# Reordering one slot and the tail of a 16-batch graph-attention kernel: turns of x1, projections, row-sum reciprocal and flag load

## The chip, the core and the metric

The kernel runs on one core of one Trainium2 chip. The metric is device time in microseconds (us) of one launch; less is better. Each time below is the median of its runs, or belongs to one profiled execution where that is said.

## The reference

There are 16 batches of 1024 rows with 256 features in float32, and a 0/1 adjacency matrix of 1024 x 1024 for each. Two layers follow each other, each with a residual and a layernorm. Cut to what matters here (the adjacency holds 0 and 1 only, so one of the four kinds of edge of layer 0 is used):

```python
# layer 0
e0    = leaky(einsum('bid,bjd->bij', h * a0[:, 0], h))      # slope 0.2
alpha = sigmoid(where(adj == 1, e0, -max))                  # kinds 2, 3, 4 likewise, with a1, a2, a3
x     = layernorm(x + einsum('bij,bjd->bid', alpha, h) + bias)
# layer 1
Hh     = einsum('bni,io->bno', x, W)
s, d   = Hh @ a_src, Hh @ a_dst
e      = where(adj != 0, exp(-leaky(s[:, :, None] + d[:, None, :])), 0)
rowsum = where(sum(e, -1) == 0, 1, sum(e, -1))
x      = layernorm(x + elu(einsum('bnm,bmo->bno', e, Hh) / rowsum))
```

## The kernel before

`one_kind_pass` does the work for an adjacency of zeros and ones. On the way it counts, in the tiles `chk` and `fit`, whether that assumption held; at the end the counts become one integer, `flag`, every engine loads it into a register, and `general_pass`, a second program for other adjacencies, runs behind `tc.If(n_bad > 0)`. Here it never runs: every engine takes the branch past it.

The order of work on each engine is the order in which the lines are written (`tc.manual_schedule`, line 79). Each engine runs its queue strictly in that order, and waits at an instruction whose input is not there; the queue of SP, which issues nearly all transfers, and the queue of POOL work in the same way. So "moved up" means: put ahead of other instructions of the same queue.

A batch of 1024 rows is 8 tiles of 128. Per batch there are these pieces:

- `strip(b, jt)` (line 191): scores of row tile jt against the tiles from jt on (the matrix is symmetric), on TensorE (PE) into a PSUM tile `pe`, then two tanh on ScalarE (ACT, lines 213 and 214) into `tb` (four buffers) and `low` (two buffers), and their maximum on VectorE (DVE, line 215).
- `finish` (line 217) masks the strip into `al`. `dump` (line 233) transposes the strip in blocks of 32 x 32 on DVE (line 237) and writes it to device memory in 4 transfers (line 241); `gather` (line 243) reads it back as the mirrored half; `mask` (line 249) masks that half (line 252).
- `sum0(b, t)` (line 305): 8 matmuls of `al` against `x` for one row tile, then bias and statistics on DVE. `center` gives the layernorm's scale and offset on POOL: `rstd` (line 276, six small operations, one of them a power) and two operations more (`mr`, lines 296 and 297). `scale0` applies them on ACT (line 301), giving the new x1.
- `save_x1(b, g)` writes one half (512 rows) of x1 to device memory (line 338); `fetch_x1(b, g)` reads it back in 32-column blocks with 8 transfers (line 112); `turn_x1(b, g)` transposes 32 x 32 blocks in place on DVE (line 349). Together they give x1 transposed, `x1T`.
- `project(b, t)` (line 351): `x1T` times `W` on PE (line 365), then three ACT operations (lines 373 to 375). Tiles 0 to 3 need the first half of x1T, tiles 4 to 7 the second. `share_p` and `weights` (line 409, on DVE) build the attention weights `e`.
- `sum1(b, t, acc, m)` (line 416): one matmul of 8 for a row tile of layer 1. `elu(b, t)` (line 424) takes the row sum out of PSUM, makes its reciprocal on DVE (lines 431, 433, 434) and applies it on ACT (lines 436, 437); `add` (line 439) adds the residual and takes statistics on DVE; `scale1` normalizes on ACT (line 301), `store` writes out (line 451).

The batches overlap in slots. Slot b (line 491) holds first the 8 strips of batch b with the 8 projections of batch b-1 between them, then 8 `sum0` of batch b, then 8 `sum1` of batch b-1. Batch 0's strips and `sum0` come before the loop, so slot 1, the second, is the only one whose previous batch has its x1 saved and fetched just before, and it has its own order: line 498 says which projections follow which strip, lines 501 to 511 where scale0, save, fetch and turn of batch 0 stand.

```python
            projects = [[], [], [], [], [0, 1], [2, 3], [], [4, 5, 6, 7]]
            if prev == 0 and jt in (3, 6):
                turn_x1(0, (jt - 3) // 3)
```

In the other slots the two turns of batch b stand at `t == 4` of the `sum1` loop and after that loop (line 580). After the loop over slots, lines 585 to 629 finish the last batch: three row tiles of `sum1` are accumulated together, m by m, as the weights come (lines 587 to 595); five more follow one by one; layernorm and stores are cut into pieces of 3, 3 and 2 tiles. Line 981 loads the flag.

## Time and profile before

| what | us |
|---|---|
| median of 3 runs | 1307.55 (1306.74 to 1307.65) |
| the profiled execution's own time | 1307.63 |
| its span in the profile | 1305.8 |
| TensorE busy in the span | 1268.1 (97%) |
| VectorE busy | 941.3 (72%) |
| ScalarE busy | 652.5 (50%) |
| GpSimd (POOL) busy | 304.2 (23%) |

The span is 1.8 us shorter than the time of the run it was taken in. In the profile PE is TensorE, and PEld its weight loads, which overlap the matmuls; DVE is VectorE, ACT ScalarE, and a q behind an engine's name its sequencer, which waits, branches and issues transfers. The granted clock of TensorE is 0.99 over the span. A busy share of 97% is a mean over stages: the first 6 us and the last 16 us hold no matmul of the loop, and the rest of the idle time lies in few places.

### The profile page before, as it was taken

The numbers are of one execution on the slowest core, as the hardware profiler recorded it, in microseconds if no ns is written. First come the engines' busy times: TensorE is split into PE (matmuls) and PEld (weight loads), VectorE is DVE, ScalarE is ACT, GpSimd is POOL, SyncE is SP. The second block draws the span as 40 slices with busy tenths as digits, with TensorE's granted clock in tenths as the row PEclk, the third lists the DMA queues.
The fourth block names the chain that finished last, engine by engine and source line by source line (L and its number), as shares of the span: only waits on it lengthen the run. The fifth ranks groups of instructions, "written<-read, shape, count | busy, mean of one in ns | idle before, by whom it ended". The sixth has DMA issues, their size and how long they took to land. (4 is left out here: it accounts for less than half of the span.)

```text
span 1305.8 us, 17594 instructions
## 1 busy us (share of the span) xinstructions
PE 1268.1 (97%) x5445; PEld 1024.2 (78%) x5445; DVE 941.3 (72%) x2126; ACT 652.5 (50%) x1461; POOL 304.2 (23%) x608
## 2 busy tenths in 40 slices
PE   7979999999999999999999999999999999999995
PEld 5758788787887878788787887878788787887874
DVE  5566786868868686786868868687786868768664
ACT  4543544645445464545645445464445635446434
POOL 2213121322212223121322213223121322213213
PEclk9989999999999999999999999999999999999998
DMA  9385497694857948488594866958488594866201
GB/s 215 64 179 108 89 193 143 128 194 84 183 122 166 186 91 192 90 182 160 114 201 84 191 121 144 195 95 201 81 181 170 111 196 76 194 135 140 72 15 68
DMA packets 609158, 181.30 MB, mean 139 GB/s; under 512 B 486184, under 2 KB 591648, under 8 KB 609056
## 3 DMA queue, kind: packets, MB, share of 16 engines
q1 hardware_dynamic: 588464, 138.61, 48.9%
q0 software_dynamic: 20592, 41.48, 17.9%
q8 instruction: 46, 0.75, 0.2%
q14 instruction: 56, 0.46, 0.1%
HBM read 152.44 MB, written 61.14 MB: 164 GB/s over the span
## 5 line engine op out<-in xcount | busy, mean ns | idle before, releaser
L312 PE MATMUL acc<-x,al 128*128 128x256 f32 x2048 | 449.3, 380 | 5.2 <-DVE al L252 5.2
L416 PE MATMUL acc<-H,e 128*128 128x257 f32 x2048 | 448.7, 380 | 1.4 <-DVE e L409 1.4
L312 PEld LDWEIGHTS acc<-x,al 128*128 128x128 f32 x2048 | 386.4, 190 | 62.7 <-DVE al L252 10.8
L416 PEld LDWEIGHTS acc<-H,e 128*128 128x128 f32 x2048 | 387.9, 190 | 59.3 <-DVE e L409 2.2
L205 PE MATMUL pe<-xa,xT 128*128 128x384 f32 (+3 forms) x768 | 267.8, 487 | 0.0
L205 PEld LDWEIGHTS pe<-xa,xT 128*128 128x128 f32 x768 | 142.2, 190 | 87.4 <-issue 45.9
L301 ACT ACTIVATE x<-x,mr,r 128x256 f32<-128x256 f32 x128 | 69.2, 592 | 231.4 <-POOL mr L297 231.4
L280 POOL TENSOR_SCALAR ve<-mv 128x4 f32<-128x4 f32 (+3 forms) x51 | 17.7, 347 | 699.0 <-DVE mv L274 698.8
L409 DVE SCALAR_TENSOR_TENSOR e<-p,pq,adj 128x1024 f32<-128x1024 f32 x128 | 159.7, 1270 | 20.1 <-DMA p<-p_row 17.2
L436 ACT ACTIVATE h<-acc,rinv 128x256 f32<-128x256 f32 x128 | 60.2, 470 | 202.5 <-DVE rinv L434 191.8
L213 ACT ACTIVATE tb<-pe 128x512 f32<-128x512 f32 (+1 forms) x192 | 94.3, 491 | 109.6 <-PE pe L205 80.0
L365 PE MATMUL pH<-Wx,x1T 128*128 128x258 f32 x512 | 131.1, 392 | 7.6 <-DVE x1T L349 4.3
L431 DVE COPY rs<-acc 128x1 f32<-128x1 f32 x128 | 20.2, 158 | 162.1 <-PE acc L416 161.6
L365 PEld LDWEIGHTS pH<-Wx,x1T 128*128 128x128 f32 x512 | 100.4, 197 | 45.2 <-issue 14.0
L215 DVE TENSOR_TENSOR tb<-tb,low 128x512 f32<-128x512 f32 (+1 forms) x192 | 101.8, 543 | 45.4 <-ACT low L214 24.6
L120 ACT ACTIVATE junk<-adj,minus 128x2048 bf16<-128x2048 bf16 x64 | 127.3, 1990 | 0.0
L231 POOL TENSOR_TENSOR al<-ident,al 128x128 f32<-128x128 f32 x128 | 60.0, 472 | 212.3 <-DVE al L221 212.1
L221 DVE SCALAR_TENSOR_TENSOR al<-tb,adj 128x512 f32<-128x512 f32 (+7 forms) x132 | 97.5, 739 | 5.0
L320 DVE SCALAR_TENSOR_TENSOR x<-acc,bias_bc 128x256 f32<-128x256 f32 x128 | 54.0, 422 | 62.4 <-PE acc L312 62.2
L214 ACT ACTIVATE low<-pe 128x512 f32<-128x512 f32 (+1 forms) x192 | 93.2, 485 | 0.8 <-DVE tb L215 0.8
L282 POOL TENSOR_TENSOR r<-ve,power 128x4 f32<-128x4 f32 (+3 forms) x51 | 79.2, 1552 | 4.2
L237 DVE STREAM_TRANSPOSE tb<-tb 128x896 f32<-128x896 f32 (+6 forms) x105 | 74.7, 712 | 3.6
(62 smaller groups left out, 938.0 us busy)
## 6 DMA issues: line engine op xcount, KB each, us to landing
adj<-in_adjT POOLq DMA_DIRECT2D x30, 1024.0 KB, 9.5
x_rows<-x SPq DMA_DIRECT2D x32, 512.0 KB, 3.4
x1T<-x_rows SPq DMA_DIRECT2D x256, 64.0 KB, 2.4
x<-in_x SPq DMA_DIRECT2D x15, 1024.0 KB, 5.8
xT<-in_x SPq DMA_DIRECT2D x120, 128.0 KB, 3.5
out<-y SPq DMA_DIRECT2D x30, 512.0 KB, 3.8
p<-p_row POOLq DMA_DIRECT2D x15, 512.0 KB, 4.2
mir<-tb SPq DMA_DIRECT2D x60, 112.0 KB, 2.4
```

Source lines behind the costliest of these rows:

```text
L120: nc.scalar.activation(junk, rows, AF.Square, bias=minus1, scale=2.0, accum_out=chk[:, b * CHECKS + n : b * CHECKS + n + 1],)
L205: nc.tensor.matmul(pe[:, 0:w], lhsT=xTs[b][:, c, ts(jt, P)], rhs=xas[b][:, c, ds(jt * P + o, w)], start=(c == 0), stop=(c == ND - 1),)
L213: nc.scalar.activation(tb[:, ds(o, w)], pe[:, 0:w], AF.Tanh, scale=0.5)
L214: nc.scalar.activation(low[:, 0:w], pe[:, 0:w], AF.Tanh, scale=0.5 * SLOPE)
L215: nc.vector.tensor_tensor(tb[:, ds(o, w)], tb[:, ds(o, w)], low[:, 0:w], ALU.max)
L221: nc.vector.scalar_tensor_tensor(als[b][:, jt, c0:c1], tbs[b, jt][:, c0 - jt * P : c1 - jt * P], 1.0, adjs[b, jt // HT][:, jt % HT, c0:c1] ...
L237: nc.vector.transpose(tb, tb)
L282: nc.gpsimd.tensor_tensor(r, ve, power[:, 0:n_t], ALU.pow)
L312: nc.tensor.matmul(acc, lhsT=als[b][:, jt, ts(t, P)], rhs=xs[b][:, jt, :], start=(jt == 0), stop=(jt == NT - 1),)
L365: nc.tensor.matmul(pt, lhsT=x1Ts[b][:, c, ts(t, P)], rhs=Wx[:, c, :], start=(c == 0), stop=(c == ND - 1),)
L409: nc.vector.scalar_tensor_tensor(es[b][:, m, :], p_bcs[b], pqs[b][:, m, 1:2], adjs[b, m // HT][:, m % HT, :], ALU.mult, ALU.min)
L416: nc.tensor.matmul(acc, lhsT=es[b][:, m, ts(t, P)], rhs=Hs[b][m], start=(m == 0), stop=(m == NT - 1),)
```

## The change

In slot 1 the first turn of x1 goes ahead of the first strip, scale0 and save of the second half go from after the second strip to after the first, and projections 0 to 3 go to one each behind strips 1 to 4. In all other slots but the last, the second turn goes from after the `sum1` loop to its step 6. The row sum is no longer copied out of PSUM: one maximum with a tiny constant reads it there. In the last batch four row tiles are accumulated together in place of three, one weights step moves behind the step it was ahead of, the flag is computed at step 5 of the last loop, its load stands ahead of the last store, the last tile's relu and normalization are done on VectorE, so that its two `mr` operations on POOL fall away, and its store is split in two.

```diff
+    TINY = 1.0e-36
-        rs = small.tile([P, 1], F32, tag="rs", name=f"rs_{b}_{t}")
-        nc.vector.tensor_copy(rs, acc[:, D : D + 1])
         rinv = small.tile([P, 1], F32, tag="rinv", name=f"rinv_{b}_{t}")
-        nc.vector.scalar_tensor_tensor(rinv, rs, 0.0, rs, ALU.is_equal, ALU.add)
+        nc.vector.tensor_scalar(rinv, acc[:, D : D + 1], TINY, None, ALU.max)
         nc.vector.reciprocal(rinv, rinv)
-        nc.scalar.activation(hs[b, t], acc[:, 0:D], AF.Relu, scale=rinv)
+        if (b, t) == (B - 1, NT - 1):
+            nc.vector.tensor_scalar(hs[b, t], acc[:, 0:D], rinv, 0.0, ALU.mult, ALU.max)
+        else:
+            nc.scalar.activation(hs[b, t], acc[:, 0:D], AF.Relu, scale=rinv)
...
-            projects = [[], [], [], [], [0, 1], [2, 3], [], [4, 5, 6, 7]]
+            projects = [[], [0], [1], [2], [3], [], [], [4, 5, 6, 7]]
+            turn_x1(0, 0)
         for jt in range(NT):
             strip(b, jt)
-            if prev == 0 and jt == 1:
+            if prev == 0 and jt == 0:
                 for t in range(HT, NT):
                     scale0(0, t)
                 save_x1(0, 1)
...
-            if prev == 0 and jt in (3, 6):
-                turn_x1(0, (jt - 3) // 3)
+            if prev == 0 and jt == 6:
+                turn_x1(0, 1)
...
             if last and t == 7:
                 weights(b, 0)
-                weights(b, 1)
             elu(prev, t, acc)
             if last and t == 7:
-                weights(b, 2)
+                weights(b, 1)
...
+            if not last and t == 6:
+                turn_x1(b, 1)
...
         if not last:
-            turn_x1(b, 1)
             add(prev, NT - 1)
...
-    first = [acc1(last, t, ps_e, "e") for t in range(3)]
+    n_first = 4
+    first = [acc1(last, t, *((ps_e, "e") if t < 3 else (ps_t, "t"))) for t in range(n_first)]
     for m in range(NT):
-        if m >= 3:
+        if m >= 2:
             weights(last, m)
...
+    nc.vector.tensor_reduce(any_bad, bad, AX.X, ALU.max)
+    flag = const.tile([1, 1], I32, tag="flag", name="flag")
...
+        if t == 5:
+            total = ps_t.tile([P, HT, P], F32, tag="t", name="total")[0:1, 0, 0:1]
+            nc.tensor.matmul(total, lhsT=any_bad, rhs=ones, start=True, stop=True)
         elu(last, t, acc)
...
+        if t == 5:
+            nc.vector.tensor_copy(flag, total)
...
+    t = NT - 1
+    add(last, t)
+    for q in range(3, t):
         scale1(last, q)
         if q == 5:
             store(last, 3, 3)
-    r1s[last] += center(mv1s[last][:, 7:8, :], f"1_{last}_7")
-    scale1(last, 7)
-    store(last, 6, 2)
+        elif q == 6:
+            store(last, 6, 1)
+    mv = mv1s[last][:, t : t + 1, :]
+    r = rstd(mv, f"1_{last}_{t}")
+    n_bad = nc.values_load(
+        flag, min_val=0, max_val=P, skip_runtime_bounds_check_because="a number of partitions"
+    )
+    y = ys[last][:, t, :]
+    nc.vector.tensor_scalar(y, y, mv[:, 0, 0:1], r, ALU.subtract, ALU.mult)
+    store(last, t, 1)
+    return n_bad
```

The computation of the flag is taken out of `tile_adj_resnorm_kernel` with this.

More of the change, by code (lines that the diff above doesn't have):

```diff
@@ L41, in one_kind_pass @@
     fit: bass.AP,
-):
+) -> bass.RuntimeValue:
     nc = tc.nc
@@ L139, in one_kind_pass @@
     nc.vector.memset(minus1, -1.0)
+    ones = const.tile([P, 1], F32, tag="ones", name="ones")
+    nc.vector.memset(ones, 1.0)
     warm = const.tile([P, 1], F32, tag="warm", name="warm")
@@ L593, in one_kind_pass @@
             r1s[done] = center(mv1s[done], f"1_{done}")
-        for t in range(3):
+        for t in range(n_first):
             sum1(last, t, first[t], m)
     check_pq(last)
+    n_chk, n_fit = chk.shape[1], fit.shape[1]
+    bad = const.tile([P, n_chk + n_fit], F32, tag="bad", name="bad")
+    nc.vector.tensor_scalar(bad[:, 0:n_chk], chk, float(NT * N // CHECKS), None, ALU.is_gt)
+    nc.vector.tensor_scalar(bad[:, n_chk:], fit, 0.5, None, ALU.is_lt)
+    any_bad = const.tile([P, 1], F32, tag="any_bad", name="any_bad")
+    nc.vector.tensor_reduce(any_bad, bad, AX.X, ALU.max)
+    flag = const.tile([1, 1], I32, tag="flag", name="flag")
     for t in range(NT):
-        if t < 3:
+        if t < n_first:
             acc = first[t]
@@ L606, in one_kind_pass @@
             add(last, t - 1)
+        if t == 5:
+            nc.vector.tensor_copy(flag, total)
         if t == 6:
             add(last, t)
-        if t in (3, 6):
-            r1s[last] += center(mv1s[last][:, ds(t - 3, 3), :], f"1_{last}_{t - 3}")
-        if t == 7:
-            add(last, t)
+        if t in (4, 6):
+            r1s[last] += center(mv1s[last][:, ds(0 if t == 4 else 3, 3), :], f"1_{last}_{t}")
         if t == 6:
@@ L622, in one_kind_pass @@
             store(last, 0, 3)
-    for q in range(3, 7):
+    t = NT - 1
+    add(last, t)
+    for q in range(3, t):
         scale1(last, q)
@@ L967 @@
         fit = flagp.tile([P, B], F32, tag="fit", name="fit")
-        one_kind_pass(tc, x, adjT, a0, bias, W, a, out, chk, fit)
-        with tc.tile_pool(name="flag_ps", bufs=1, space=PSUM) as flag_ps:
-            bad = flagp.tile([P, NCHK + B], F32, tag="bad", name="bad")
-            nc.vector.tensor_scalar(bad[:, 0:NCHK], chk, float(N // P * N // CHECKS), None, ALU.is_gt)
-            nc.vector.tensor_scalar(bad[:, NCHK:], fit, 0.5, None, ALU.is_lt)
-            any_bad = flagp.tile([P, 1], F32, tag="any_bad", name="any_bad")
-            nc.vector.tensor_reduce(any_bad, bad, AX.X, ALU.max)
-            ones = flagp.tile([P, 1], F32, tag="one", name="one")
-            nc.vector.memset(ones, 1.0)
-            total = flag_ps.tile([1, 1], F32, tag="total", name="total")
-            nc.tensor.matmul(total, lhsT=any_bad, rhs=ones, start=True, stop=True)
-            flag = flagp.tile([1, 1], I32, tag="flag", name="flag")
-            nc.vector.tensor_copy(flag, total)
-        n_bad = nc.values_load(flag[0:1, 0:1], min_val=0, max_val=P)
+        n_bad = one_kind_pass(tc, x, adjT, a0, bias, W, a, out, chk, fit)
         with tc.If(n_bad > 0):
```

## The prediction

> **What bounds the kernel now.** I read the page's busy shares first, then the waits of PE, then the timelines of the two places where PE waits, and last the end of the span on POOL. Everything is taken from one profiled execution of 1307.63 us (span 1305.8, so 1.8 us lie around it); the median of the runs is 1307.55, the same within 0.08. I give the new time on the scale of 1307.63.

> ```profile
> PE 1268.1 (97%) x5445; PEld 1024.2 (78%) x5445; DVE 941.3 (72%) x2126; ACT 652.5 (50%) x1461; POOL 304.2 (23%) x608
> ...
> PE acc L312 <- DVE al L252: 5.2, 14, 0.4
> PE pH L365 <- DVE x1T L349: 4.3, 1, 4.3
> PE pH L365 <- DMA mir<-tb: 3.1, 1, 3.1
> ...
> PE acc L416 <- DVE e L409: 1.4, 2, 0.9
> ```

> PE has 97%, so DVE, ACT or POOL work taken away elsewhere is worth nothing unless PE waits for it. It waits in four ways that the change can touch: 0.4 us in each of 14 slots (L252), 4.3 and 3.1 us once each in slot 1, and 1.4 us in the m-loop of the tail. The first one stays: the mask follows a strip that waits for PE itself (DVE is idle for 1.86 us at 639.1 before L215), so a shorter DVE queue does not bring it forward.

> Slot 1 on PE's timeline (start, length, operation, count, idle before):

> ```profile
> 58.29 13.12 PE L205 MATMUL pe<-xa,xT 128*128 128x512 f32 x36
> 75.72 3.63 PE L365 MATMUL pH<-Wx,x1T 128*128 128x258 f32 x8 [4.31 <-DVE x1T L349]
> ...
> 86.76 6.65 PE L365 MATMUL pH<-Wx,x1T 128*128 128x258 f32 x16 [3.06 <-DMA mir<-tb]
> 93.73 0.28 PE L391 MATMUL prow<-ident,pq 128*8 128x128 f32 x1 [0.32 <-ACT pq L374]
> ```

> Strips and projections take 58.29 to 93.85, 35.6 us, against 22.6 us (621.51 to 644.09) in a slot of the middle: 13 us are lost here. The second wait is named after a transfer, but what ends last is the turn of the second half on DVE (L349, 85.35 to 86.55). Beside the idle time there is the clock, in PE's windows (us, busy, granted clock, DMA share, GB/s):

> ```profile
> 77.00:78.00 1.00, 1.00 (x3) 0.50 0.75 114
> ...
> 90.00:91.00 1.00, 1.00 (x4) 0.50 0.72 179
> ```

> The clock is halved for 3.4 us from 75.6 and for 6.8 us from 85.9, so the 16 matmuls at 86.76 take 6.65 us; the same 16 at full clock take 3.75 (1252.13). Then SP's queue:

> ```profile
> 66.23 2.17 SPq L241 DMA_DIRECT2D mir<-tb  x4
> 68.50 0.55 SPq L338 DMA_DIRECT2D x_rows<-x  x1
> 69.41 2.61 SPq L241 DMA_DIRECT2D mir<-tb  x4
> 72.11 4.26 SPq L112 DMA_DIRECT2D x1T<-x_rows  x8
> 76.47 0.43 SPq L245 DMA_DIRECT2D al<-mir  x1
> 77.01 3.14 SPq L241 DMA_DIRECT2D mir<-tb  x4
> ```

> From 66.23 it issues without a pause. It is to be seen that 17 transfers stand between the start of dump 1 and the end of dump 2, and that they fill the time up to 80.15.

> At the end, POOL:

> ```profile
> 1288.44 0.32 POOL L280 TENSOR_SCALAR ve<-mv 128x3 f32<-128x3 f32 x1 [6.79 <-DVE mv L274]
> ...
> 1296.49 0.19 POOL L296 TENSOR_TENSOR mr<-mv,r 128x1 f32<-128x1 f32 x1
> 1296.76 0.23 POOL L297 TENSOR_SCALAR mr<-mr 128x1 f32<-128x1 f32 x1
> ...
> L981 POOLq TENSOR_LOAD <-flag x1: 498/498/498, 1296.7 to 1296.7; - x1
> ...
> L982 POOLq INC_SWDGE_SEM  x1: 632/632/632, 1302.5 to 1302.5; - x1
> ```

> POOL works without a pause from 1288.44 to 1296.99 (three chains of a layernorm), loads the flag, branches at 1297.33 and only goes on at 1299.96; after 1302.5 come a drain (to 1305.0) and the barrier. SP has seen the last store land at 1300.8 and waits for POOL. POOL sets the end; the last store has 2.2 us to spare.

> [...]

> **Row sum (L431 to L434).** 128 copies of 158 ns fall away, 20.2 us of DVE, and the compare with two sources becomes a maximum from PSUM, a read like the copy's. In the slots DVE is not what PE waits for, so nothing follows. In the tail it is 0.2 us on the way to POOL.

> **turn_x1(b, 1) at step 6 of sum1.** The same 1.25 us operation in 14 slots, two steps earlier, ahead of the DVE part of the last two elu. DVE is idle for about 1.47 us just there (620.24 to 621.71). It waits for the fetch behind it; the last landing comes 1.65 us before in slot 1, 1.98 in slot 3, 2.4 to 4.5 in the others. Cost 0.

> **Slot 1.** *First turn.* It stands ahead of strip 0 in DVE's queue. Its fetch (8 transfers of L112 from 53.92) has landed by 60.83, and DVE's timeline has nothing from 59.6 to 61.33: turn from 60.95 to 62.2, the second L215 starts at 63.04 as before, the first is late by 0.9 us without anyone waiting. Cost 0. With it projections 0 to 3 run between the strips at full clock; the 4.31 us of idle time and the slow 3.63 us are gone, but PE then reaches the end of its strips at about 77.5 and stands still until the second turn. So only the second turn counts. *scale0* (four on ACT, 2.06 us) starts when POOL has the offsets, 63.24, to 65.35, ahead of tanh operations that then come late: dump 1 becomes ready about 0.46 us later, 69.87. *save* then runs at 65.4 in a free stretch of SP instead of in the full one. Dump 1 takes 2.1 (a middle slot, 633.52 to 635.62) to 2.6 us. The fetch behind it so shifts by s = -0.05 to +0.46. *Then* the same 17 transfers; dump 2's last landing moves from 82.24 to 82.24 + s. The buffer `tb` is one of four, so tanh of strip 6 waits for that landing: 82.4 + s, against 83.29 now, when PE's slow projections held it. From there to the turn DVE takes what it takes now (tanh at 83.29, turn at 85.35), less about 0.2 since mask 0 is done by then: PE starts at 82.4 + 0.2 + 3.1 = 85.6 to 86.1 against 86.76, a gain of 0.65 to 1.15; I take 0.8. *Clock*: PE has then idled for 8 us and starts cold. It leaves half speed after 3.4 to 6.8 us[...]: the 16 matmuls take 3.5 + half of that, 5.2 to 6.7, middle 5.95, against 6.65: -0.7. Together -1.5, bounds -0.4 to -2.6.

> **Tail, PE.** Four accumulators instead of three mean 4 x 0.435 us of matmuls per m, so that `e` (L409, 1.27 us each) is due later. Laid out again with the durations of the DVE rows, the second `e` (now behind the elu's reciprocal, 1260.32 to 1261.59) is 0.04 us late and the third (behind add, 1262.98 to 1264.25) 0.92, 0.96 together, where the same count gives 1.83 now (0.56 and 0.87 by the record, the rest inside the groups); with 0.1 for the flag's matmul, which goes from behind the last row tile to ahead of it, the last row tile ends 0.75 us earlier. **Tail, POOL.** Its chain for tiles 3 to 5 starts with row tile 5's add, so 0.75 + 0.2 (row sum) earlier, and stays without a pause; the last two `mr` operations fall away (1296.49 to 1296.99, less the overlap with the load: 0.54). The branch comes 1.5 us earlier. [...] **Tail, DVE.** Tile 7's relu on DVE reads PSUM: 0.42 us (by L442, two sources), against 0.47 on ACT; POOL needs tile 7's statistics at 1293.5, and has them at about 1291.5. [...] I take 0.42 against 0.60 on ACT: store at about 1295.95, seen by SP at about 1299, 2.6 us ahead of POOL. Cost and gain 0, and none for splitting the store. The flag's load on the other engines stands in waits for POOL's r. Sum -1.5.

> **Sum:** 1307.63 - 1.5 - 1.5 = 1304.6.

> **Rivals.** *A, slot 1 gives nothing*: the queue of SP is later than I think[...]: 1307.63 - 1.5 = 1306.1. For it: the same transfers, a clock that depends on chance. Against it: tanh 6 was held by PE, not by SP. *B, SP was not the limit*: once PE no longer delays strips 4 to 6, transfers land faster, and the second turn follows its own fetch (landed by 78.2) more closely, some 5 us earlier: 1299.6. Against it: dump 2 issues without a pause. *C, slower*: turn_x1(b, 1) at step 6 stands ahead of the elu of the last row tiles; if its fetch lands late in the slots, DVE's queue waits, and after it strip 0's L215 and PE. It has 1.65 us or more of margin, and DVE 1.86 us of idle time at strip 4, so it decides from about 4.2 us of delay; 5 us late in 14 slots would give 14 x 0.8 = 11, thus about 1316. For it: nothing in the landing times; only that removed DVE work and earlier turns could bunch the transfers.

> **How the numbers follow.** Forecast 0.73, A 0.12, B 0.08, C 0.07. A measurement of this kernel tells 0.2% (2.6 us) from no change, that is 1304.9. The forecast's own range is 1303 to 1306.4; a little over half of it, 0.44, lies below 1304.9. Faster 0.44 + 0.08 = 0.52, same 0.29 + 0.12 = 0.41, slower 0.07. The range takes in A and POOL's gap: 1302.4 to 1307.2; B and C are left out.

> **What would show it.** Right: in slot 1 no wait before projections 0 to 3, one wait of about 8 us before 4 to 7 that begins at about 77.5, PE at 85.6 to 86.1, sum0 at 91.5 to 92.8 instead of 93.85; slots of 78.7 us as now; POOL's branch 1.5 us earlier against the last matmul's old place, and POOL still last. Wrong: L349 waiting on L112 in the slots, sum0's start near 89 or after 93.8, or the last store behind POOL.

## The result, and the profile after

The changed kernel takes 1303.37 us (median of 10 runs, 1302.71 to 1304.77) against 1307.18 (10 runs, 1306.02 to 1308.07) for the kernel before on the same chip: 3.8 us less, ratio 0.9973 with a 95% interval of 0.9963 to 0.9982. The forecast was 1304.6.

The profiled execution of the changed kernel was the longest of its ten: 1304.77, span 1303.0. It is 2.86 us shorter than the profiled one of before, not 3.8; what differs from execution to execution is found below. Lines were added to its code, so the numbers have moved, many by three: L312 is L315 now, L365 is L368, L409 is L412, L349 is L352, L241 is L244; the fetch, L112, is L113.

The waits of PE (line, releaser, us in total, times, longest):

```profile
PE pH L368 <- issue: 8.4, 1, 8.4
...
PE acc L315 <- DVE al L255: 5.3, 14, 0.4
...
PE acc L419 <- DVE e L412: 0.6, 1, 0.6
```

The two waits of slot 1 (4.3 and 3.1) have become one of 8.4 us. The 14 waits in front of sum0 are untouched, and of the tail's two waits one is left. PE's timeline of slot 1:

```profile
63.74 1.03 PE L368 MATMUL pH<-Wx,x1T 128*128 128x258 f32 x4
...
72.97 1.03 PE L368 MATMUL pH<-Wx,x1T 128*128 128x258 f32 x4
73.85 2.76 PE L208 MATMUL pe<-xa,xT 128*128 128x384 f32 x12
85.05 6.54 PE L368 MATMUL pH<-Wx,x1T 128*128 128x258 f32 x16 [8.45 <-issue]
91.92 0.28 PE L394 MATMUL prow<-ident,pq 128*8 128x128 f32 x1 [0.33 <-ACT pq L377]
92.03 3.25 PE L315 MATMUL acc<-x,al 128*128 128x256 f32 x14
```

Projections 0 to 3 run between the strips at full clock (4 instructions, two for each matmul, in 1.03 us), PE is through with the strips at 76.6, and then stands still until projections 4 to 7. sum0 starts at 92.03 instead of 93.85, of which 0.99 us were there before slot 1 began (first strip at 57.30 instead of 58.29). The wait is put down to "issue", so it is DVE's timeline that says what ended it:

```profile
77.54 0.45 DVE L240 STREAM_TRANSPOSE tb<-tb 128x256 f32<-128x256 f32 x1
79.85 1.16 DVE L255 SCALAR_TENSOR_TENSOR al<-al,adj 128x384 f32<-128x384 f32 x2 [1.87 <-DMA al<-mir]
82.60 0.42 DVE L218 TENSOR_TENSOR tb<-tb,low 128x256 f32<-128x256 f32 x1 [1.58 <-ACT low L217]
83.06 0.42 DVE L224 SCALAR_TENSOR_TENSOR al<-tb,adj 128x256 f32<-128x256 f32 x1
83.51 0.31 DVE L240 STREAM_TRANSPOSE tb<-tb 128x128 f32<-128x128 f32 x1
83.75 1.20 DVE L352 STREAM_TRANSPOSE x1T<-x1T 128x1024 f32<-128x1024 f32 x1
```

The turn (L352) is ready to run at 77.6, when the last block of its fetch lands, and DVE is idle from 77.98 to 79.85 and again from 81.0 to 82.6. It runs at 83.75, because strip 6 stands ahead of it and waits for its buffer (ACT's L216 of strip 6 starts at 81.91, after 5.70 us of waiting for `mir<-tb`). SP's queue, where the buffer's release comes from, is full as before:

```profile
64.98 0.38 SPq L341 DMA_DIRECT2D x_rows<-x  x1
65.45 6.07 SPq L244 DMA_DIRECT2D mir<-tb  x8
71.57 4.31 SPq L113 DMA_DIRECT2D x1T<-x_rows  x8
75.98 0.43 SPq L248 DMA_DIRECT2D al<-mir  x1
76.51 3.12 SPq L244 DMA_DIRECT2D mir<-tb  x4
```

The save now stands ahead of dump 0, and dumps 0 and 1 follow each other. The fetch starts at 71.57 instead of 72.11; counted from the first strip that is 14.27 us instead of 13.82, so in this execution it is later, not earlier. At the end, POOL (its timeline, then the operations of the branch's line, with their shortest, middle and longest duration in ns):

```profile
1285.46 0.32 POOL L283 TENSOR_SCALAR ve<-mv 128x3 f32<-128x3 f32 x1 [4.17 <-DVE mv L277]
...
1293.40 0.19 POOL L291 TENSOR_TENSOR r<-r,n 128x1 f32<-128x1 f32 x1
```

```profile
L998 POOLq EVENT_SEMAPHORE  x5: 17/43/43, 1296.9 to 1299.5; - x5
...
L998 POOLq COMPARE_BRANCH  x1: 45/45/45, 1293.9 to 1293.9; - x1
...
L998 POOLq INC_SWDGE_SEM  x1: 636/636/636, 1299.6 to 1299.6; - x1
```

The last two operations of the chain are gone and POOL branches at 1293.92 instead of 1297.29, 3.4 us earlier; but from there to the semaphore operation (INC_SWDGE_SEM) it takes 5.69 us instead of 5.19. Cut into stretches, the two profiled executions compare so (us, from PE's and POOL's instructions in the traces; the last matmul, counted to its end, is that of row tile 7):

| stretch | before | after | difference |
|---|---|---|---|
| start to first strip of slot 1 | 58.29 | 57.30 | -0.99 |
| slot 1, first strip to sum0 | 35.55 | 34.73 | -0.82 |
| a middle slot (mean of 12) | 78.689 | 78.683 | -0.006 |
| last slot, its strips to projections 0 to 3 of batch 15 | 72.10 | 71.90 | -0.20 |
| projections 4 to 7 of batch 15 to the last matmul | 37.65 | 36.96 | -0.69 |
| last matmul to POOL's branch | 7.51 | 6.93 | -0.58 |
| branch to INC_SWDGE_SEM | 5.19 | 5.69 | +0.50 |
| from there to the end | 3.36 | 3.37 | 0 |

### The profile page after: what moved, and what is told of

Same layout as the page of the kernel before. It is cut to its first block, busy times and chain, and to the rows that moved or that the text cites. A ratio compares the mean times of both kernels' runs of the same rounds, so it can differ in the third digit from the quotient of the medians.

```text
span 1303.0 us, 17447 instructions
## 1 busy us (share of the span) xinstructions
PE 1265.0 (97%) x5445; PEld 1022.0 (78%) x5445; DVE 925.4 (71%) x2000; ACT 650.7 (50%) x1459; POOL 295.3 (23%) x606
## 4 chain that ended last, share of the span: by engine, by line
PE 82%; issue 5%; SPq 4%; DVE 4%; DMA 3%; POOL 1%; ACT 1%; POOLq 0%; DVEq 0%
PE acc L315 34%; PE acc L419 30%; PE pe L208 13%; PE pH L368 4%; SPq L244 3%; DMA mir<-tb 2%; DVE al L224 1%; DVE tb L240 1%; DVE tb L218 1%; ACT tb L216 1%; DVE al L255 1%; POOL r L285 1%; ACT low L217 0%; DMA x<-in_x 0%; SPq L248 0%
## 5 line engine op out<-in xcount | busy, mean ns | idle before, releaser
L315 PE MATMUL acc<-x,al 128*128 128x256 f32 x2048 | 449.3, 380 | 5.3 <-DVE al L255 5.3
L315 PEld LDWEIGHTS acc<-x,al 128*128 128x128 f32 x2048 | 386.4, 190 | 62.8 <-DVE al L255 10.9
L412 DVE SCALAR_TENSOR_TENSOR e<-p,pq,adj 128x1024 f32<-128x1024 f32 x128 | 159.8, 1270 | 20.8 <-DMA p<-p_row 17.8
L216 ACT ACTIVATE tb<-pe 128x512 f32<-128x512 f32 (+1 forms) x192 | 94.3, 491 | 117.2 <-PE pe L208 78.5
L368 PE MATMUL pH<-Wx,x1T 128*128 128x258 f32 x512 | 129.4, 387 | 8.5 <-issue 8.4
L435 DVE TENSOR_SCALAR rinv<-acc 128x1 f32<-128x1 f32 x128 | 20.1, 157 | 162.2 <-PE acc L419 162.1
L368 PEld LDWEIGHTS pH<-Wx,x1T 128*128 128x128 f32 x512 | 99.1, 194 | 45.5 <-issue 22.9
L234 POOL TENSOR_TENSOR al<-ident,al 128x128 f32<-128x128 f32 x128 | 68.2, 533 | 241.2 <-DVE al L224 241.0
L255 DVE SCALAR_TENSOR_TENSOR al<-al,adj 128x512 f32<-128x512 f32 (+3 forms) x150 | 76.5, 534 | 1.9 <-DMA al<-mir 1.9
```

The costliest lines, as they stand in the source:

```text
L216: nc.scalar.activation(tb[:, ds(o, w)], pe[:, 0:w], AF.Tanh, scale=0.5)
L255: nc.vector.scalar_tensor_tensor(v, v, 1.0, rows, ALU.add, ALU.mult)
L315: nc.tensor.matmul(acc, lhsT=als[b][:, jt, ts(t, P)], rhs=xs[b][:, jt, :], start=(jt == 0), stop=(jt == NT - 1),)
L368: nc.tensor.matmul(pt, lhsT=x1Ts[b][:, c, ts(t, P)], rhs=Wx[:, c, :], start=(c == 0), stop=(c == ND - 1),)
L412: nc.vector.scalar_tensor_tensor(es[b][:, m, :], p_bcs[b], pqs[b][:, m, 1:2], adjs[b, m // HT][:, m % HT, :], ALU.mult, ALU.min)
```

## The experiments

All were timed in five rounds beside the kernel before, whose median was 1306.96, 1306.88 and 1307.09 in the three groups.

**Slot 1 alone, and everything else alone.**

```diff
-            projects = [[], [], [], [], [0, 1], [2, 3], [], [4, 5, 6, 7]]
+            projects = [[], [0], [1], [2], [3], [], [], [4, 5, 6, 7]]
+            turn_x1(0, 0)
...
-            if prev == 0 and jt == 1:
+            if prev == 0 and jt == 0:
...
-            if prev == 0 and jt in (3, 6):
-                turn_x1(0, (jt - 3) // 3)
+            if prev == 0 and jt == 6:
+                turn_x1(0, 1)
```

This on the kernel before:

> The kernel before with the three edits of slot 1 alone (first turn ahead of strip 0, scale0 and save behind strip 0, projections 0 to 3 behind strips 1 to 4). Theory (slot 1 is worth the earlier second turn only, the clock little): slot 1 from its first strip to sum0 takes 34.7 us instead of 35.6, time 0.5 to 1.5 us below before, and the tail's POOL branch stands against the last matmul as in before. Rival (all of the 3.8 us comes from slot 1): 3 us or more below before.

1304.94 us, ratio 0.9984 (0.9977 to 0.9991): about 2 us, more than the 0.5 to 1.5 expected and less than the rival's 3. Slot 1 takes 32.84, not 34.7. The reverse of this diff on the changed kernel:

> The changed kernel with the order of slot 1 put back. Theory: keeps the gain of the tail, about 0.7 on PE, 0.6 on POOL and 0.2 in the last slot[...]: 1.2 to 2.2 us below before, and slot 1 at 35.6 us. Rival (slot 1 is all): as before. Rival (parts help each other): more than 3 us below before.

1305.69, ratio 0.9991 (0.9983 to 0.9999): 1.3 us; slot 1 at 35.58. So about 2 us are slot 1 and 1.3 the rest, and they add up to the whole within the noise (3.2 us for the changed kernel in the same rounds, next).

**The changed kernel again.**

> The changed kernel once more, to see what differs from execution to execution. Theory: the 1.0 us by which its first profile was ahead of before's at the first sum0, before any edit acts, and the 0.5 us by which POOL's gaps behind its branch were longer, are chance: one or both come out different here by 0.2 us or more, while slot 1 (34.7), the middle slots (78.68) and the stretch from the last strips to the last matmul (37.0) agree within 0.3. Rival: the changed program starts faster because it is shorter or laid out otherwise: first sum0 at 24.5 again, and gaps of 2.9 and 2.4 again.

1303.78, ratio 0.9977 (0.9966 to 0.9987). The first strip of slot 1 is at 58.09 this time, so the head start of 1 us is chance. The fetch of slot 1 begins at 71.57 in one execution and 71.59 in the other, so the first had lost its head start again by then. POOL's stretch from the branch to INC_SWDGE_SEM is 5.51 again (5.69 in the first), so that it is longer than before is not chance. Slot 1 does not agree, against what was expected: 33.00 against 34.73, sum0 at 91.09 against 92.03. The middle slots (78.68) and the stretch to the last matmul (36.95) do. PE's windows of the two (us, busy, granted clock, DMA share, GB/s), first the one profiled first, then this one:

```profile
85.00:88.00 3.00, 2.95 (x7) 0.50 1.06 225
88.00:91.00 3.00, 3.00 (x9) 0.54 0.49 102
91.00:92.00 1.00, 0.68 (x4) 1.00 0.32 82
```

```profile
85.00:88.00 3.00, 3.00 (x8) 0.50 1.05 216
88.00:89.00 1.00, 1.00 (x4) 0.50 0.27 48
89.00:90.00 1.00, 1.00 (x6) 0.96 0.87 204
```

In the first the clock is half from 80.53 to 90.77, three times 3.41 us; in this one from 82.26 to 89.08, twice 3.41. PE begins at 85.05 and 84.83, so it works at half speed for 5.7 us in the one and 4.3 in the other. At a clock of 0.50 half of that difference, 0.7 us, is lost time. The other 1.0 of the 1.73 us came earlier: PE began 27.75 us after the first strip in the first execution and 26.74 in this one, since the save, and behind it the fetch, were later there (7.68 and 14.27 us after the first strip, against 6.70 and 13.50). The first profile had the worse draw in both.

The kernel before varies too. Of its 98 executions in the five rounds, 87 took 1305.9 to 1308.9 us and 11 took 1303.6 to 1304.1, these at a mean clock of 0.994 instead of 0.991 or 0.992. So one execution in nine of the old kernel is as short as the new one, and only medians of many tell them apart. Less time at half clock would fit the higher mean, but none of the eleven was profiled.

**Is it scale0 and the save?** One edit put back in the changed kernel:

```diff
-            if prev == 0 and jt == 0:
+            if prev == 0 and jt == 1:
                 for t in range(HT, NT):
```

> The changed kernel with scale0 and the save of the second half back behind strip 1; the first turn and the projections stay where the change puts them. Theory (the second turn comes earlier because PE's slow projections no longer hold strip 6, and the moved save spares SP 0.5 us at most): projections 4 to 7 still begin at 84.5 to 85.8 us of the span, sum0 at 90.4 to 92.8, within 1 us of the changed kernel. Rival (scale0 and save moved up are what brings the fetch and so the turn forward): projections 4 to 7 at 86.5 or later, and 2 us or more above the changed kernel.

1304.14 (ratio 0.9982, 0.9975 to 0.9989), projections 4 to 7 at 84.20, 27.05 us after the first strip and so among the other executions, sum0 at 89.84. Moving scale0 and save brings nothing that can be measured; the first turn and the projections, taken together, do it: strip 6 no longer stands behind slow matmuls on PE (8 instructions of the projections in 3.63 us before, at a clock of 0.50 up to 79.06; 4 in 1.03 now).

**The second turn's place.** The turn one strip earlier:

```diff
-            if prev == 0 and jt == 6:
+            if prev == 0 and jt == 5:
                 turn_x1(0, 1)
```

> The changed kernel with the second turn of slot 1 behind strip 5 instead of strip 6 in DVE's queue. Its fetch had landed 17 transfers' worth early, at 77.60, and DVE stood idle from 77.98 to 79.85. Theory (the turn is late only because it stands behind strip 6, whose buffer waits for dump 2): turn at 78.0, projections 4 to 6 on PE at about 79.3 instead of 85.05; projection 7 and sum0 then wait for ACT, whose share of projections 4 to 7 stands behind tanh 7 (85.1): sum0 at about 87.5 instead of 92.0, 4 to 5 us below the changed kernel. Rival (SP's transfers bound the slot, not the place of the turn): sum0 at 91 or later, within 1 us of the changed kernel.

The mechanism came as expected: projections 4 to 6 at 79.80, sum0 at 87.33. But the time is 1301.50 (ratio 0.9959, 0.9946 to 0.9973), only about 2 us below the changed kernel, half of the 4 to 5 expected. PE's timeline and windows:

```profile
79.80 4.54 PE L368 MATMUL pH<-Wx,x1T 128*128 128x258 f32 x12 [3.34 <-issue]
85.75 1.14 PE L368 MATMUL pH<-Wx,x1T 128*128 128x258 f32 x4 [1.41 <-ACT H L376]
87.21 0.28 PE L394 MATMUL prow<-ident,pq 128*8 128x128 f32 x1 [0.32 <-ACT pq L377]
87.33 25.00 PE L315 MATMUL acc<-x,al 128*128 128x256 f32 x107
```

```profile
80.00:84.00 4.00, 4.00 (x12) 0.57 0.96 197
84.00:88.00 4.00, 2.27 (x9) 0.92 1.00 213
88.00:92.00 4.00, 4.00 (x13) 0.65 0.43 95
```

The clock is half from 80.57 to 83.99, whole for 3.41 us, and half again from 87.40 to 90.81, now under sum0; in the 3.41 us between, PE was busy for 1.68, and its waits for ACT there were 1.41 and 0.32. The 3.41 us at a clock of 0.50 cost half of their length, 1.7, of what was gained; and against the slot of 33.00 us in e3 this one's 30.01 is only 3.0 shorter, so the comparison with the first profile (34.73) had promised too much. With the fetch ahead as well, so that PE need not wait:

```diff
-            projects = [[], [0], [1], [2], [3], [], [], [4, 5, 6, 7]]
+            projects = [[], [0], [1], [2], [3], [4, 5], [6, 7], []]
...
-            if prev == 0 and jt == 1:
+            if prev == 0 and jt == 0:
                 fetch_x1(0, 1)
-            if prev == 0 and jt == 6:
+            if prev == 0 and jt == 3:
                 turn_x1(0, 1)
```

> The changed kernel with slot 1 ordered once more: the fetch of the second half right behind dump 0 (ahead of dump 1 in SP's queue), the second turn behind strip 3, projections 4 to 7 two each behind strips 5 and 6. Theory (only the place in the queues makes the second turn late, and the idle time it causes is what halves the clock): fetch landed by 75, turn by 76, PE without a wait of over 2 us from the first strip to sum0 and no stretch of half clock, sum0 23 to 25 us after the first strip instead of 33 to 34.7: 8 to 10 us below the changed kernel, about 1294. Rival (the transfers of dump 1 and dump 2, now behind the fetch, hold up the strips or the masks for sum0): the time comes back as waits of sum0 for L255, and less than 5 us is gained.

1295.17 us, ratio 0.9910 (0.9897 to 0.9924), 8.2 below the changed kernel's first median, as expected. PE's timeline:

```profile
75.58 1.98 PE L368 MATMUL pH<-Wx,x1T 128*128 128x258 f32 x8 [0.60 <-PE pe L208]
77.40 1.02 PE L208 MATMUL pe<-xa,xT 128*128 128x256 f32 x4
78.26 1.91 PE L368 MATMUL pH<-Wx,x1T 128*128 128x258 f32 x8
80.01 0.61 PE L208 MATMUL pe<-xa,xT 128*128 128x128 f32 x4
81.61 0.28 PE L394 MATMUL prow<-ident,pq 128*8 128x128 f32 x1 [1.00 <-ACT pq L377]
81.73 27.85 PE L315 MATMUL acc<-x,al 128*128 128x256 f32 x128
```

Slot 1 takes 24.58 us, near the 22.6 of a middle slot, and the clock is never halved between 8.5 us and the last matmul (mean over the span 0.996, against 0.992 in the changed kernel). The transfers put behind the fetch hold nothing up: the 128 instructions of batch 1's sum0 follow each other from 81.73 without a gap.

**The wait in front of sum0.**

```diff
-            if jt >= 5:
+            if jt == 4:
+                mask(b, 0)
+            if jt >= 6:
                 mask(b, jt - 5)
```

> The changed kernel with the mask of strip 0's mirrored half behind strip 4 instead of strip 5 in DVE's queue, in all slots. Theory (the 0.37 us in front of sum0 in each of 14 slots is set by that mask's place behind strips that PE itself paces, not by the amount of DVE work; so the removed row-sum copies could not shorten it): the wait for L255 (5.3 us in 14 pieces) is gone, slots of 78.3 instead of 78.68 us, 5 us below the changed kernel, about 1298.5. Rival (DVE's queue is full there, so that what is pulled ahead makes strip 5 or mask 1 late): slots of 78.6 or more.

1294.98, ratio 0.9907 (0.9891 to 0.9922): 8.4 us below the changed kernel, more than the 5 expected. The wait is gone from the list, and a slot takes 78.04 instead of 78.68. What one wait cost was thus 0.64 us, not the 0.38 that its line shows. PE's timeline of the changed kernel at one of them:

```profile
642.23 0.60 PE L315 MATMUL acc<-x,al 128*128 128x256 f32 x2
643.21 9.12 PE L315 MATMUL acc<-x,al 128*128 128x256 f32 x41 [0.38 <-DVE al L255]
```

Back to back these instructions start every 0.216 us and last 0.379. The second starts at 642.45, the third at 643.21: 0.76 instead of 0.216, so 0.54 are lost, and the fourth is late by 0.10 more. The 0.38 runs from the end of an instruction, which overlaps the next one when they are not held up. Both edits together (the mask of slot 1 left where it was):

> Both: slot 1 as in e5, and the earlier mask in the slots behind it. Theory: the two gains add up, 13 to 15 us below the changed kernel, about 1289. Rival (they share a resource): less than 11 us.

1286.31, ratio 0.9841 (0.9828 to 0.9855): 20.6 us below the kernel before and 17 below the changed one, more than the 13 to 15 expected. The gains measured one by one, 8.2 and 8.4, add up to it.

**Row sum and the middle slots' turn.** The copy of the row sum back, and `turn_x1(b, 1)` back behind the loop:

```diff
+        rs = small.tile([P, 1], F32, tag="rs", name=f"rs_{b}_{t}")
+        nc.vector.tensor_copy(rs, acc[:, D : D + 1])
...
-        nc.vector.tensor_scalar(rinv, acc[:, D : D + 1], TINY, None, ALU.max)
+        nc.vector.scalar_tensor_tensor(rinv, rs, 0.0, rs, ALU.is_equal, ALU.add)
...
-            if not last and t == 6:
-                turn_x1(b, 1)
...
         if not last:
+            turn_x1(b, 1)
             add(prev, NT - 1)
```

> The changed kernel with the copy of the row sum (158 ns, 128 times) back in and the second turn of x1 back behind the sum1 loop. Theory: nothing in the middle slots (78.68 to 78.69 us), 0.2 us later at POOL's branch, together at most 0.5 us above the changed kernel. Rival (20 us less of DVE work and the earlier turn carry part of the gain): slots longer by 0.1 us or more, 1.5 us or more above the changed kernel.

1304.47, ratio 0.9981 (0.9973 to 0.9989). The middle slots stay at 78.683. Against the changed kernel the last slot is 0.19 longer (72.09), the stretch to the last matmul 0.28 (37.24) and POOL's branch 0.20 later (7.13): 0.67 in all, a little over what was expected and far from the rival; by the medians it is 1.1, or 0.7 against the second measurement. And the turn one step earlier still:

```diff
-            if not last and t == 6:
+            if not last and t == 5:
                 turn_x1(b, 1)
```

> The changed kernel with the second turn of x1 at step 5 of sum1 in the middle slots, one step earlier still. Its fetch's last landing is about 0.5 us behind the end of the work ahead of it there (616.38 against 615.84), so DVE waits in front of the row sum of row tile 6. Theory (DVE has slack to the next strips): slots stay at 78.68 us, the turn waits 0.3 to 1 us in every slot, and the time is within 0.5 us of the changed kernel. Rival (a turn that waits for its fetch holds up DVE, then the strips and PE): slots longer by 0.1 us or more, 1.5 us or more above the changed kernel.

1303.94, ratio 0.9975 (0.9965 to 0.9985), middle slots 78.684. DVE's waits, here and, in the second line, in the changed kernel:

```profile
DVE x1T L352 <- DMA x1T<-x_rows: 8.9, 18, 1.9
```

```profile
DVE x1T L352 <- DMA x1T<-x_rows: 3.3, 10, 1.2
```

DVE waits 8.9 us for fetches in place of 3.3, up to 1.9 at once, and PE notices nothing. The waits stand in 5 of the 14 slots (0.37 to 1.85 us), not in every slot as expected; in the other 9 the fetch had landed.

**The tail.** Three row tiles together in place of four, with the weights step back ahead of elu:

```diff
+                weights(b, 1)
             elu(prev, t, acc)
             if last and t == 7:
-                weights(b, 1)
+                weights(b, 2)
...
-    n_first = 4
+    n_first = 3
...
-        if m >= 2:
+        if m >= 3:
```

> The changed kernel with three row tiles accumulated together in the last batch and the weights step back ahead of elu. Theory: from the last strips to the last matmul 37.5 to 37.7 us instead of 36.96, so 0.6 to 0.8 us above the changed kernel. Rival (the shorter row-sum chain on DVE alone makes the weights come in time): 37.2 or less.

1304.86, ratio 0.9984 (0.9978 to 0.9991); the stretch to the last matmul takes 37.67, 0.71 more, as the theory had it; by the medians it is 1.1 to 1.5. Last, the final tile's `mr` on POOL and its normalization on ACT:

```diff
-    r = rstd(mv, f"1_{last}_{t}")
+    r1s[last] += center(mv, f"1_{last}_{t}")
...
-    y = ys[last][:, t, :]
-    nc.vector.tensor_scalar(y, y, mv[:, 0, 0:1], r, ALU.subtract, ALU.mult)
+    scale1(last, t)
```

> The changed kernel with the last tile's two mr operations on POOL back, and its normalization on ACT. Theory: POOL's branch 0.54 us later against the last matmul (7.47 instead of 6.93). For the stretch from branch to the last semaphore operation, 5.46 to 6.20 in the runs with the changed tail against 4.98 and 5.19 with the old one: [...] it is 5.2 or less here, since DVE branches 3 us earlier, and the time stays within 0.3 us of the changed kernel; if it is something else in the program, it stays at 5.4 or more, and the time is 0.5 us above.

1302.14, ratio 0.9959 (0.9946 to 0.9972): by the medians 1.2 to 1.6 us faster than the changed kernel, though the intervals of the two ratios overlap. POOL's branch is 7.43 behind the last matmul, 0.5 later, as both theories had it. What follows:

```profile
L997 POOLq EVENT_SEMAPHORE  x5: 17/43/43, 1296.6 to 1296.9; - x5
...
L997 DVEq COMPARE_BRANCH  x1: 72/72/72, 1289.7 to 1289.7; - x1
...
L997 POOLq COMPARE_BRANCH  x1: 45/45/45, 1293.7 to 1293.7; - x1
...
L997 POOLq INC_SWDGE_SEM  x1: 636/636/636, 1297.0 to 1297.0; - x1
```

From branch to INC_SWDGE_SEM 3.32 us. By its number that is what the theory that DVE's branch, 0.3 us ahead of POOL's in the changed kernel, lengthens the stretch asked for, but it is not what happened. The first gap behind the branch (1293.71 to 1296.55) is 2.85, as in the changed kernel (2.88), although DVE branches 3.9 us ahead of POOL here. It is the second gap, 2.39 us between the second and the third semaphore instruction in the changed kernel, that is gone: the five follow each other from 1296.6 to 1296.9. With 0.5 later at the branch that makes 1.9 us less.

What made the second gap is not shown. In the changed kernel two packets of the DMA queue of kind "instruction" begin in it, 3.20 and 3.81 us behind the branch; here two begin at 3.13 and 3.49, while POOL's five instructions stand at 2.89 to 3.23. That POOL waited for those packets in the changed kernel was the author's guess: the edit puts two more instructions on POOL ahead of the branch, but it also takes an operation from DVE to ACT, and no run moved the code alone. Nor is it shown why the first gap is longer with the changed tail (2.85 to 3.46 us in twelve profiles) than with the old one (2.57 and 2.63): DVE's early branch does not shorten it, and its cause stays open.

## Why the prediction was right

**Slot 1, the second turn.** Right in its mechanism: one wait of 8 us from about 77, ended by the turn, which is released through strip 6's buffer by dump 2. For its size, 0.65 to 1.15 us with 0.8 taken, the times have to be counted from the first strip, since that came 0.99 us earlier by chance in the first profile. PE began 28.47 us after it before and 27.75 in the first profile: 0.72 less, as forecast. In seven more executions with this order it began after 26.74 to 27.51, a gain of 0.96 to 1.73, beyond the range in five. What differs is the shift s of the fetch, taken as -0.05 to +0.46. The fetch began 13.82 us after the first strip before; it began 14.26 or 14.27 in three executions (s = +0.45, the first profile among them) and 13.44 to 13.67 in five (s = -0.15 to -0.38). Dump 1 took 2.10 us in all eight, the lower end of what was counted, but began later by 0.17 to 0.40 us in the five and by 1.0 in the three, where 0.46 was counted for scale0.

**Slot 1, the clock.** That PE would start at half speed and need 3.4 to 6.8 us to leave it, an estimate from the lengths of the two halved stretches of before, is what the traces show: 5.7 and 4.3 us in the two executions of the changed kernel, 3.5 in e1. The first profile shows next to nothing of the 0.7 (6.98 from projection 4 to sum0, 7.09 before), e3 and e1 show 0.8 and 1.2 (6.26 and 5.89). The forecast's longest time for the 16 matmuls, 3.5 and half of 6.8, is 6.9, not 6.7; its bounds for the slot have the 6.9. Together slot 1 was forecast at 1.5 and is worth about 2 by the times of e1, within the bounds of 0.4 to 2.6; from first strip to sum0 the eight executions gained 0.8 to 2.8.

**The first turn, scale0, save, the fetch.** The first turn waits 1.24 us for its fetch, and nothing waits for it; e9 gives scale0 and save no measurable worth. Rival A (slot 1 gives nothing) falls with e1. Rival B (second turn 5 us earlier) was wrong about what the change does, but e4 shows that its sentence "SP was not the limit" is right: the turn stands behind a strip that SP holds up, and is not held up itself.

**Row sum, middle slots.** Nothing, as forecast (78.689 to 78.683). The waits in front of sum0 stayed, and e6 bears out why: they hang on the mask's place in DVE's queue. At step 6 the turn stands ahead of one elu, not two, which changes nothing. Rival C falls: e12 puts the turn yet earlier, DVE waits, PE does not. Costed at nothing but worth 0.2 us was the last slot. There the first turn stands behind the row sums in DVE's queue, and the projection behind it came 0.21 us late (its 0.2 us are gone from the list of waits, and back in it in e8). And e8 gives the row sum in the tail 0.28 on PE beside the 0.20 on POOL.

**Tail.** PE's 0.75 came out as 0.69. Of this e11 gives 0.71 to the four accumulators with the moved weights step, and e8 gives 0.28 to the row sum, so the two overlap. POOL's branch came 0.58 us closer to the last matmul, where 0.2 and 0.54 were counted; taken back one by one, these were 0.20 and 0.50. The gaps behind the branch, taken as unchanged with bounds of -1 to +1 (the author's estimate), cost 0.5 us: 5.46 to 6.20 in the eleven profiles with the changed tail (e10 apart), 5.19 and 4.98 in the two with the old one. So the tail gave 0.8 by the profiles, about 1 by e2, instead of 1.5. The normalization on DVE took 0.41 us where 0.42 was counted, and the relu from PSUM 0.48 for 0.42. SP had seen the last store land at 1296.9, 2.7 us ahead of POOL's semaphore operation: hidden, as said.

**The sum.** About 2 for slot 1, 0.8 to 1 for the tail and 0.2 for the last slot make 3.0 to 3.2, which is what the second measurement shows (3.2); the first showed 3.8. The forecast was 3.0. That its two errors, too little for slot 1 and too much for the tail, stand against each other is luck.

## What to carry to other kernels

An instruction that stands in a strict queue behind one with a longer wait inherits that wait: ask of every late step whether its own input is late, or only its neighbour's (here 77.6 against 83.75; worth about 2 us with the turn alone moved, and 8 with its fetch and the projections moved too). An idle stretch of PE cost more than its length here: each of 3.06 us or more in slot 1 came with a halved clock for 3.41 to 10.24 us, so a gain that leaves several short waits behind may not show. And small waits that return in every slot are worth more than they look: measure them by the distance of starts against the usual distance (0.64 us here, where the list of waits had 0.38).

## What the runs showed of the hardware

```profile
83.99:87.40 3.41, 1.68 (x8) 1.00 1.00 221
87.40:90.81 3.41, 3.41 (x10) 0.50 0.56 113
```

```profile
76.42:79.83 3.41, 1.44 (x9) 1.00 0.82 166
79.83:83.24 3.41, 0.00 (x0) 1.00 1.04 219
```

```profile
83.80:87.21 3.41, 3.01 (x7) 0.50 1.06 235
87.21:90.62 3.41, 3.08 (x15) 1.00 0.44 95
```

The clock was halved after a piece in which PE did nothing (changed kernel, 77.12 to 80.53), but also after pieces in which it was busy for 36% (before, 82.47 to 85.88) and 49% (e4) of the time, and not after pieces with 42% (e8) and 44% (e6, 76.30 to 79.71). So the busy share of a piece, as the trace shows it, does not decide alone; what does is open. A halved clock stayed after pieces with 67% (changed kernel, 83.94 to 87.35) and 74% (before, 85.88 to 89.29), and rose after pieces with 88% (e9), 98% (before, 75.65 to 79.06) and 100% (changed kernel, 87.35 to 90.77).

The end of the program lost a gap of 2.39 us behind the branch by a small edit (e10: two more instructions on POOL, one operation moved from DVE to ACT). What made the gap is not shown. Whether e7 with that edit would gain the same was not tried.
